# Tap spectra in steps of twelve output channels instead of eight

## The chip, the cores and the metric

The kernel runs on one core of a Trainium2 chip. The metric is device time in microseconds (us), the median of several runs. One further execution was recorded by the hardware profiler; all rows shown here come from its trace. The engines are named as the profile names them: PE (TensorE matmul) and PEld (its weight loads), DVE (VectorE), ACT (ScalarE), POOL (GpSimd) and SP (SyncE, which here only issues DMAs). Everything is fp32, and an fp32 matmul stands in the trace as two instructions (two passes).

## The reference, cut to what matters

There are two graph layers over 128 graphs of 128 nodes with 256 channels. The part that concerns the change is the convolution over 17 nodes in layer 0:

```python
h = relu(layernorm(x))                       # x: (128, 128, 256)
xc = transpose(h, (0, 2, 1))
h = relu(bn(conv1d(xc, conv1_w, 0)))         # 1 tap, 256 -> 256 channels
h = bn(conv1d(h, conv2_w, 8))                # 17 taps, padding 8, 256 -> 256
x_conv = transpose(relu(h + xc), (0, 2, 1))
...
```

Its result goes with a message-passing term into a GRU-like gate, and layer 1 (five graph convolutions over subsets of the first 25 nodes) follows. None of that is touched.

## The kernel before

The 17-tap convolution is done in the frequency domain. With a transform length of LW = 136, the signal and the taps are multiplied by cosine and sine tables (`fd` for the signal, `gt` for the taps), the spectra are multiplied frequency by frequency, and the result is transformed back. The span has these stages:

- The head stage, up to about 274 us. It runs over 32 blocks of four graphs (`heads`, L264). Block i makes the layer norm of a later block on DVE (`head_stats`, `head_norm`), the first convolution (`head_conv1`, L235 on PE, L238 on DVE, `head_relu` on ACT), the transposition of block i+1 (`head_turn`, L221 on PE, L222 on ACT, stored to DRAM as `htd`), and the signal spectra of block i-1 (`head_spectra`, L251 on PE, copied at L259 by DVE and L261 by ACT into `X`).
- Between these pieces, `between()` runs one tap step. `between` is `some_spectra`, which advances the generator `weight_spectra` (L165). The taps of conv2 come in 16 groups: two halves c of the input channels by eight groups q of WCH = 32 output channels. A group's taps `w2` hold four row groups (partitions 0, 32, 64 and 96 on, 17 rows each) with eight products each. A product takes 17 rows of taps for one output channel and 128 input channels as weights and streams the 136 columns of `gt` (L172). A step before does two products in each of the four row groups, eight output channels in all; the four row groups write four different PSUM banks, two products side by side in each (272 of a bank's 512 columns). Then the four banks are copied to the tile `sp`: three by ACT (L180), the fourth by DVE (L178), except in a group's last step, where ACT takes all four. A group has four steps, the whole has 64. When the generator is advanced once more, it stores `sp` (2,176 KB) to DRAM as `vd` (L182); the taps three groups on are then loaded, and the first step of the next group runs in the same call.
- The spectral stage, to about 457 us: for each of the 68 frequency pairs, `vd` is read back as `v`, POOL sums its real and imaginary parts (L324), and PE makes three products with `X` (L316, L327, L332).
- The gates and layer 1, to the end, with L658 the greatest part of PE's work.

In the head stage the order of the instructions on each engine is the program's own (`manual_schedule`), with a few small instructions of later code placed in between (the softmax of the fusion weights `fw`, L490 to L504, is one). PSUM is used in turn: `bank()` gives the eight banks in a fixed rotation, and so each allocation waits for whatever was to be read from the bank eight allocations before. A block with two steps takes 16 banks: one for each half of conv1, four for each step, two for the transposition and four for the signal spectra.

Four calls of `some_spectra` lie ahead of `heads`; in `heads`, each block has two calls (L271 and L288), and every eighth block a third one (L291). With 64 steps the last one falls into the early call of block 28, and the late call of that block issues the last store. All loads and stores of the head stage other than two small ones are issued by SP, in program order. `sp` has two buffers, `w2` three.

Of the kernel before, what the change touches and what calls it, by code (L numbers as in the profile page):

```python
# [13 lines left out]
P = 128  # L14
EPS = 1e-5
KW = 17
PAD = 8
BB = 4
LW = P + PAD
NP_ = LW // 2  # L20
NB = 20
WCH = 32
NR = LW - P
PARTS = [40, 40, 40, 8]
NN = 25
# [49 lines left out]
def gnn_kernel(ctx: ExitStack, tc: tile.TileContext, io, out0: bass.AP, out1: bass.AP):  # L75
    nc = tc.nc
# [13 lines left out]
    def bank():  # L90
        pool, n = banks
        if n is None:
            return pool.tile([P, 512], F32, tag="bank", name="bank")
        banks[1] = (n + 1) % 8
        return pool.tile([P, 512], F32, tag=f"bank{n}", name="bank")
# [56 lines left out]
    htd = [dram.tile([P, C, T], F32, tag=f"ht{i}", name=f"htd{i}") for i in range(NBLK)]  # L152
    vd = dram.tile([C, D // WCH, P, LW, WCH], F32, tag="vd", name="vd")
    yd = dram.tile([B, P, D], F32, tag="yd", name="yd")
    yrd = dram.tile([B, NR, D], F32, tag="yrd", name="yrd")

    def taps_load(pool, c, q, queue, split=1, amid=None):
        w2 = pool.tile([P, WCH // 4, P], F32, tag="w2", name="w2", bufs=3)
        for t in range(0, WCH // 4, WCH // 4 // split):
            queue.dma_start(w2[:, t:t + WCH // 4 // split], io["w2t"][:, c, q, t:t + WCH // 4 // split])  # L160
            if amid:
                amid.pop()()
        return w2

    def weight_spectra(pool, c, q, w2):  # L165

        sp = pool.tile([P, LW, WCH], F32, tag="sp", name="sp", bufs=2)
        for t in range(WCH // 8):
            ps = [bank() for _ in range(4)]
            for j in range(2):  # L170
                for r in range(4):
                    nc.tensor.matmul(ps[r][:, j * LW:(j + 1) * LW], w2[32 * r:32 * r + KW, 2 * t + j, :],  # L172
                                     gt[32 * r:32 * r + KW, :], start=True, stop=True)
            for r in range(4):
                o0 = t * 8 + 2 * r
                dst, s = sp[:, :, o0:o0 + 2], ps[r][:, :2 * LW].rearrange("p (j d) -> p d j", j=2)
                if r == 3 and t < WCH // 8 - 1:
                    nc.vector.tensor_copy(dst, s)  # L178
                else:
                    nc.scalar.copy(dst, s)  # L180
            yield
        nc.sync.dma_start(vd[c, q], sp)  # L182
# [4 lines left out]
    def head_load(pool, ahead, i, queue):  # L187
        xs[i] = pool.tile([P, BB, D], F32, tag="ln", name="ln", bufs=ahead)
        queue.dma_start(xs[i], x[i])
# [36 lines left out]
    def head_conv1(wk, i, h):  # L226
        if not h:
            h1s[i] = wk.tile([P, BB, D], F32, tag="h1", name="h1", bufs=2)
        ht = hcs[i]
        ps = bank()  # L230
        pv = ps.rearrange("p (b d) -> p b d", b=2)
        for bb in range(2):
            b = 2 * h + bb
            for c in range(C):
                nc.tensor.matmul(pv[:, bb, :], ht[:, c, b * N:(b + 1) * N], wc1[:, c, :],  # L235
                                 start=c == 0, stop=c == C - 1)
        hv = h1s[i][:, 2 * h:2 * h + 2, :]
        nc.vector.tensor_tensor(hv, pv, sh1[:, None, :].to_broadcast([P, 2, D]), op=ALU.add)  # L238

    def head_relu(i, h):  # L240
        hv = h1s[i][:, 2 * h:2 * h + 2, :]
        nc.scalar.activation(hv, hv, AF.Relu)
# [21 lines left out]
    def heads(wk, xk, ahead, X, between, consts):  # L264

        for i in range(NBLK + 1):
            if i + ahead < NBLK:
                head_load(xk, ahead, i + ahead, nc.sync)
            if i < NBLK:
                head_conv1(wk, i, 0)  # L270
            between()  # L271
            if i < NBLK:
                head_relu(i, 0)
            if i == 0:
                head_norm(1)
            elif i + 3 < NBLK:
                head_stats(wk, i + 3, (0,))
            if i < NBLK:
                head_conv1(wk, i, 1)
            if i + 1 < NBLK:  # L280
                head_turn(wk, i + 1)
            if i < NBLK:
                head_relu(i, 1)
            if i == 0:
                head_stats(wk, 2)
            if i + 2 < NBLK:
                head_norm(i + 2)
            between()  # L288
            if i > 0:
                head_spectra(X, i - 1)  # L290
            if i % 8 == 7:  # L291
                between()
            if i + 3 < NBLK:
                head_stats(wk, i + 3, (1,) if i else (0, 1))
            if i == 2:
                next(consts)
# [180 lines left out]
    def load_y(i):  # L477
# [4 lines left out]
        for o in range(C):  # L482
            for h in range(2):
                r0, g1 = 32 * (2 * o + h), g0 + 2 * h
                nc.sync.dma_start(yr[r0:r0 + 2 * NR, :],
                                  yrd[g1:g1 + 2, :, o * P:(o + 1) * P].rearrange("g r o -> (g r) o"))
# [22 lines left out]
    def conv_out(i):  # L509
# [5 lines left out]
        for o in range(C):  # L515
            for h, ps in enumerate(pss[o]):
                r0 = 32 * (2 * o + h)
                g = slice(r0, r0 + 2 * NR)
                nc.tensor.matmul(ps, yr[g, :], idr[g, :], start=True, stop=False)  # L519
# [602 lines left out]
def _spectral_constants():  # L1122
# [28 lines left out]
    for b in range(2):  # L1151
        idr[:, b * NR:(b + 1) * NR, b] = inv[P:]
    d = {"gt": gt.reshape(P, LW), "fd": fd.reshape(P, LW), "idm": inv[:P], "idr": idr.reshape(P, 2 * P)}
# [3 lines left out]
def _lay_out(a):  # L1157

    import numpy as np

    cc = np.ascontiguousarray

    def cols(v):
        return v.reshape(-1, P).T

    w = {k[7:]: v for k, v in a.items() if k.startswith("L0_gnn_")}
    l = {k[7:]: v for k, v in a.items() if k.startswith("L1_gnn_")}
    by = (-1, BB, P)
    d = {"x": cc(a["x"].reshape(*by, 2 * P).transpose(0, 2, 1, 3)), "xT": cc(a["x"].reshape(-1, BB * P, 2, P).transpose(0, 3, 2, 1)), "adjT": cc(a["adj"].reshape(*by, P).transpose(0, 3, 1, 2))}
    d["vec"] = cc(np.concatenate(  # L1170
        [cols(w[f"bn{j}_{q}"]) for j in (1, 2) for q in "gbmv"]
        + [cols(w["b_ih"]), cols(w["b_hh"]), cols(l["b1"]), cols(l["b2"])], axis=1))
    d["wc1"] = cc(w["conv1_w"][:, :, 0].T)

    w2 = w["conv2_w"].reshape(-1, WCH // 8, 4, 2, 2, P, KW).transpose(2, 6, 4, 0, 1, 3, 5)
    d["w2t"] = np.zeros((4, 32) + w2.shape[2:], np.float32)
    d["w2t"][:, :KW] = w2
    d["w2t"] = d["w2t"].reshape(P, 2, -1, WCH // 4, P)
    d.update(_spectral_constants())
    pad = np.zeros((2 * MW - w["w_msg"].shape[0] - 3, w["w_msg"].shape[1]), np.float32)  # L1180
    d["wms"] = cc(np.concatenate([w["w_msg"], w["w_se"], pad]).T)
    d["bms"] = cc(np.concatenate([w["b_msg"], w["b_se"], pad[:, 0]]))
    d["wih"] = cc(w["w_ih"].T)
    d["whh"] = cc(w["w_hh"].T)
    d["w1"] = cc(l["W1"])
    d["w2"] = cc(l["W2"])
    d["fw"] = cc(l["fusion_w"])
    sub = []
    for s, runs in GROUPS:
        idx = [r0 + j for r0, rn in runs for j in range(rn)]  # L1190
        sub.append((idx, a["adj"][:, idx][:, :, idx]))
    nblk = a["adj"].shape[0] // BB

    e = np.zeros((nblk, BB, NN, GW), np.float32)
    ie = np.zeros((BB, NN, GW), np.float32)
    bl = np.zeros((nblk, BB, NN, GW // BB), np.float32)
    fl = np.zeros((nblk, GW, NN), np.float32)
    for g, (idx, ad) in enumerate(sub):
        s = len(idx)
        ad = ad.reshape(nblk, BB, s, s)  # L1200
        for b in range(BB):
            c0 = GOFF[g] + b * s
            e[:, b, idx, c0:c0 + s] = ad[:, b].transpose(0, 2, 1)
            ie[b, idx, c0 + np.arange(s)] = 1.0
            fl[:, c0:c0 + s, :s] = ad[:, b]
            bl[:, b, idx, GOFF[g] // BB:GOFF[g] // BB + s] = ad[:, b]
    d["adjE"] = e.reshape(nblk, BB * NN, GW)
    d["ie"] = ie.reshape(BB * NN, GW)
    d["adjB"] = cc(bl.reshape(nblk, BB * NN, GW // BB).transpose(1, 0, 2))
    d["adjF"] = cc(fl.reshape(-1, P, NN).transpose(1, 0, 2))  # L1210

    d["adjN"] = np.zeros((len(PACKS), P, P), np.float32)
    d["adjK"] = np.zeros((P, len(PACKS), NN), np.float32)
    for j, (k, (g, b0, nb)) in enumerate(PACKS):
        s = len(sub[g][0])
        for b in range(nb):
            ad = sub[g][1][sum(PARTS[:k]) + b0 + b]
            d["adjN"][j, b * s:(b + 1) * s, b * s:(b + 1) * s] = ad.T
            d["adjK"][b * s:(b + 1) * s, j, :s] = ad
    return d  # L1220
# [22 lines left out]
```

## Time and profile before

| | us |
|---|---|
| median of 3 runs | 1865.76 (1865.35 to 1867.79) |
| the profiled execution | 1866.29 |
| its span, first to last instruction | 1864.5 |
| outside the span | 1.8 |
| head stage (to the first L316 product) | 273.6 |
| PE busy in the tap steps (L172), 1,024 instructions | 50.6 |
| ACT busy in the copies of the tap steps (L180), 208 | 67.0 |
| DVE busy in the copies of the tap steps (L178), 48 | 21.0 |

Busy times of a group are unions: where instructions overlap, the time counts once. The chain of waits is followed back from the last instruction to what released each step; its rows are start, length and the work. A row of PE matmuls in the timeline counts instructions, so that `x16` at L172 is a step of eight products in two passes each. The mean granted clock of TensorE over the span is 0.997: two short stretches ran at half clock, 33.45 to 36.86 us and 456.7 to 463.5 us, and PE's first products (up to about 20 us) take twice as long as later ones though the granted clock in the records is 1.0 there.

### The profile page before, as it was taken

Reading aid. Unit: us, or ns where it says so; the run is one execution under the profiler, and the core shown is the slowest. Engines: PE = TensorE matmul, PEld = TensorE weight load, DVE = VectorE, ACT = ScalarE, POOL = GpSimd, SP = SyncE. Lnnn points to the kernel's source line nnn. Section 1 sums busy time; section 2 is a strip of 40 time slices with the busy share of each in tenths; the row PEclk is TensorE's granted clock in tenths of the full one; section 3 lists DMA queues with packets and bytes.
Section 4 is the critical chain, followed back from the end, with each engine's and each line's share of the span. In section 5 each row is a group of like instructions: output and inputs, shape, how many; then the busy total and the mean of one; then the engine's idle time right before and its main releaser. Section 6 shows DMA issues by size and latency. Waiting matters only on the chain.

```text
span 1864.5 us, 31417 instructions
## 1 busy us (share of the span) xinstructions
PE 1843.8 (99%) x10982; PEld 1592.3 (85%) x10982; DVE 1361.9 (73%) x3312; ACT 737.0 (40%) x1668; POOL 652.9 (35%) x803
## 2 busy tenths in 40 slices
PE   8999999999999999999999999999999999999998
PEld 6888888887888888888888888888888888888887
DVE  6888865555988888888656778888756788888643
ACT  4666651111443334333334433433343343334334
POOL 1111125675343544454321345444412243544200
PEclk9999999999999999999999999999999999999999
DMA  8788778997532233224234422333232433222125
GB/s 294 285 303 334 302 277 285 344 325 244 171 88 75 72 85 94 76 73 124 73 90 119 120 75 72 88 83 113 61 103 85 131 95 87 73 72 70 39 89 158
DMA packets 219420, 267.98 MB, mean 144 GB/s; under 512 B 106210, under 2 KB 182967, under 8 KB 217215
## 3 DMA queue, kind: packets, MB, share of 16 engines
q1 hardware_dynamic: 214079, 248.04, 42.8%
q10 hardware_dynamic: 5184, 17.93, 2.4%
q8 instruction: 88, 1.44, 0.3%
q14 instruction: 69, 0.57, 0.1%
HBM read 169.24 MB, written 96.67 MB: 143 GB/s over the span
## 4 chain that ended last, share of the span: by engine, by line
PE 90%; DVE 4%; DMA 2%; POOL 2%; SPq 1%; issue 1%; ACT 1%; ACTq 0%; DVEq 0%; POOLq 0%
PE bank L658 43%; PE bank L332 6%; PE bank L235 6%; PE bank L926 5%; PE bank L986 5%; PE bank L544 4%; PE bank L251 4%; PE bank L523 3%; PE bank L327 3%; PE bank L609 3%; PE bank L172 2%; PE bank L221 1%; PE bank L905 1%; DMA nt<-in_adjN_dram 1%; PE bank L835 1%; PE bank L519 1%
## 5 line engine op out<-in xcount | busy, mean ns | idle before, releaser
L658 PE MATMUL bank<-t,sw 128*128 128x256 f32 x1152 | 291.4, 380 | 0.0
L671 POOL TENSOR_TENSOR u<-u,m 128x256 f32<-128x256 f32 x128 | 93.7, 732 | 465.1 <-ACT m L669 386.7
L658 PEld LDWEIGHTS bank<-t,sw 128*128 128x128 f32 x1152 | 212.7, 190 | 29.0 <-issue 2.3
L658 PE MATMUL bank<-t,wih 128*128 128x256 f32 x768 | 197.2, 379 | 0.0
L658 PEld LDWEIGHTS bank<-t,wih 128*128 128x128 f32 x768 | 145.5, 190 | 20.9 <-issue 0.9
L235 PE MATMUL bank<-wc,ht 128*128 128x256 f32 x512 | 126.0, 390 | 0.0
L324 POOL TENSOR_TENSOR vs<-v 128x256 f32<-128x256 f32 x134 | 99.0, 763 | 70.9 <-DMA v<-vd 44.1
L658 PE MATMUL bank<-t,whh 128*128 128x256 f32 x384 | 117.5, 388 | 0.0
L567 ACT ACTIVATE msg<-msg 128x512 f32<-128x512 f32 x64 | 36.9, 622 | 196.7 <-DVE msg L563 196.7
L658 PE MATMUL bank<-xc,wih 128*128 128x256 f32 x384 | 114.4, 379 | 0.0
L658 PE MATMUL bank<-xn,wih 128*128 128x256 f32 x384 | 114.2, 379 | 0.0
L986 PE MATMUL bank<-w,hh 128*125 128x256 f32 (+9 forms) x480 | 113.5, 380 | 0.6 <-DVE hh L931 0.6
L658 PE MATMUL bank<-ht,whh 128*128 128x256 f32 x384 | 109.9, 380 | 0.0
L205 POOL TENSOR_TENSOR rs<-ve,mhalf 128x4 f32<-128x4 f32 x32 | 32.3, 1009 | 217.0 <-DVE ve L203 209.9
L926 PE MATMUL bank<-ax,w 128*128 128x500 f32 (+8 forms) x416 | 107.0, 396 | 0.1
L235 PEld LDWEIGHTS bank<-wc,ht 128*128 128x128 f32 x512 | 93.8, 193 | 15.1 <-issue 0.3
L986 PEld LDWEIGHTS bank<-w,hh 128*125 128x125 f32 (+9 forms) x480 | 84.3, 178 | 18.8 <-DVE hh L931 1.0
L180 ACT COPY sp<-bank 128x272 f32<-128x272 f32 x208 | 67.0, 408 | 68.7 <-PE bank L172 52.9
L676 DVE TENSOR_TENSOR u<-bank,u 128x256 f32<-128x256 f32 x128 | 53.7, 420 | 54.6 <-PE bank L658 53.0
L321 DVE SCALAR_TENSOR_TENSOR s<-X 128x256 f32<-128x256 f32 x67 | 45.0, 672 | 64.9 <-PE bank L332 64.9
L669 ACT COPY m<-bank 128x256 f32<-128x256 f32 x128 | 47.3, 369 | 104.5 <-PE bank L658 104.5
L926 PEld LDWEIGHTS bank<-ax,w 128*128 128x128 f32 x416 | 69.9, 190 | 19.4 <-issue 12.3
(206 smaller groups left out, 4415.8 us busy)
## 6 DMA issues: line engine op xcount, KB each, us to landing
vd<-sp SPq DMA_DIRECT2D x16, 2176.0 KB
v<-vd SPq DMA_DIRECT2D x34, 1024.0 KB
w<-in_w_dram SPq DMA_DIRECT2D x40, 512.0 KB
ln<-in_x_dram SPq DMA_DIRECT2D x32, 512.0 KB
htd<-ht SPq DMA_DIRECT2D x32, 512.0 KB
yd<-ys ACTq DMA_DIRECT2D x32, 512.0 KB
ht<-htd SPq DMA_DIRECT2D x32, 512.0 KB
ym<-yd SPq DMA_DIRECT2D x32, 512.0 KB
```

Source lines behind the costliest of these rows:

```text
L180: nc.scalar.copy(dst, s)
L235: nc.tensor.matmul(pv[:, bb, :], ht[:, c, b * N:(b + 1) * N], wc1[:, c, :], start=c == 0, stop=c == C - 1)
L251: nc.tensor.matmul(ps[:, bb * LW:(bb + 1) * LW], h1[:, 2 * h + bb, c * P:(c + 1) * P], fd, start=True, stop=True)
L324: nc.gpsimd.tensor_tensor(vs[:, c], vr[c], vi[c], op=ALU.add)
L327: nc.tensor.matmul(p1[:, :D], a[:, c], vs[:, c], start=c == 0, stop=c == C - 1)
L332: nc.tensor.matmul(ps[:, k * D:(k + 1) * D], u[:, c], w[c], start=c == 0, stop=c == C - 1)
L523: nc.tensor.matmul(ps[:, b * N:(b + 1) * N], ym[:, 2 * h + b, o * P:(o + 1) * P], idm, start=False, stop=b == 1)
L544: nc.tensor.matmul(ps[:, b, :], d[:, b * N:(b + 1) * N], w, start=True, stop=True)
L658: nc.tensor.matmul(ps, w, d, start=n == 0, stop=n == len(pairs) - 1)
L671: nc.gpsimd.tensor_tensor(got["u4"], got["u2"], got["m5"], op=ALU.add)
L926: nc.tensor.matmul(pv[:, q - q0, :], w1s[k5 + g][:, c, q * P:(q + 1) * P], xv[:, c], start=c == 0, stop=c == C - 1)
L986: nc.tensor.matmul(ps[:n1, :D], hh[:, q, at:at + n1], w2s[k5 + g][:, q, :], start=q == 0, stop=q == HID // P - 1)
```

## The change

A step does three products in each row group, twelve output channels, and fills 408 of a bank's 512 columns. A group of eight products in each row group then has three steps, of 3, 3 and 2 products (48 steps in all, in place of 64), and its copies have 408, 408 and 272 columns. Output channels are assigned anew: row group r holds the eight consecutive channels from 8r on, so that a copy writes three (or two) neighbouring channels of `sp` for each frequency; the taps are laid out for this on the host. DVE takes the fourth bank in all but a group's last step, as before. The calls are thinned: the late call of a block runs in odd blocks and in block 0 only, and the third call of each eighth block is gone. The last step stays in the early call of block 28; the last store is then issued by the early call of block 29. The softmax of `fw` lies at other places between the early instructions of ACT and DVE, since the gaps that it is put into are others.

```diff
+STEP = 3
...
     def weight_spectra(pool, c, q, w2):
 
         sp = pool.tile([P, LW, WCH], F32, tag="sp", name="sp", bufs=2)
-        for t in range(WCH // 8):
+        n = WCH // 4
+        for s0 in range(0, n, STEP):
+            s1 = min(s0 + STEP, n)
             ps = [bank() for _ in range(4)]
-            for j in range(2):
+            for j in range(s1 - s0):
                 for r in range(4):
-                    nc.tensor.matmul(ps[r][:, j * LW:(j + 1) * LW], w2[32 * r:32 * r + KW, 2 * t + j, :],
+                    nc.tensor.matmul(ps[r][:, j * LW:(j + 1) * LW], w2[32 * r:32 * r + KW, s0 + j, :],
                                      gt[32 * r:32 * r + KW, :], start=True, stop=True)
             for r in range(4):
-                o0 = t * 8 + 2 * r
-                dst, s = sp[:, :, o0:o0 + 2], ps[r][:, :2 * LW].rearrange("p (j d) -> p d j", j=2)
-                if r == 3 and t < WCH // 8 - 1:
+                o0 = r * n + s0
+                dst = sp[:, :, o0:o0 + s1 - s0]
+                s = ps[r][:, :(s1 - s0) * LW].rearrange("p (j d) -> p d j", d=LW)
+                if r == 3 and s1 < n:
                     nc.vector.tensor_copy(dst, s)
                 else:
                     nc.scalar.copy(dst, s)
...
-            between()
+            if i % 2 or i == 0:
+                between()
             if i > 0:
                 head_spectra(X, i - 1)
-            if i % 8 == 7:
-                between()
...
-    w2 = w["conv2_w"].reshape(-1, WCH // 8, 4, 2, 2, P, KW).transpose(2, 6, 4, 0, 1, 3, 5)
+    w2 = w["conv2_w"].reshape(-1, 4, WCH // 4, 2, P, KW).transpose(1, 5, 3, 0, 2, 4)
```

## The prediction

> **What bounds the kernel now.** I read the engines' busy shares first, then the waits of PE, then the chain of waits in two stretches of the stage that the change touches, and last the rows of the tap steps.
>
> ```profile
> PE 1843.8 (99%) x10982; PEld 1592.3 (85%) x10982; DVE 1361.9 (73%) x3312; ACT 737.0 (40%) x1668; POOL 652.9 (35%) x803
> ```
>
> PE is never free. The changed code runs in the first 273.6 us (the head stage; the first product of the next stage, L316, starts at 273.57). The waits of PE in the whole span are few (the columns: microseconds in total, times, the longest), and those of the head stage lie nearly all in its first 34 us (of the two at L251, 0.6 ends at 33.5 and 0.4 at 51.7):
>
> ```profile
> PE bank L172 <- DMA gt<-in_gt_dram: 3.4, 1, 3.4
> ...
> PE bank L140 <- DVE bnb L136: 2.8, 1, 2.8
> PE bank L172 <- DVE h L238: 2.0, 1, 2.0
> PE bank L251 <- DVE h L238: 1.0, 2, 0.6
> ...
> PE bank L172 <- ACT sp L180: 0.5, 1, 0.5
> ```
>
> After 33.5 us the head stage is a row of PE work, so a PE microsecond removed there is a microsecond of the span. The chain of waits shows one block with two tap steps (L172):
>
> ```profile
> 99.71 2.05 PE bank L251 x16
> 101.77 1.73 PE bank L235 x8
> 103.49 0.68 PE bank L172 x16
> 104.17 1.92 PE bank L235 x8
> 106.09 0.87 PE bank L221 x8
> 106.97 0.68 PE bank L172 x16
> 107.64 2.05 PE bank L251 x16
> ```
>
> and, when the steps have run out, a block without any:
>
> ```profile
> 251.39 1.85 PE bank L251 x16
> 253.25 3.45 PE bank L235 x16
> 256.70 0.87 PE bank L221 x8
> 257.57 1.86 PE bank L251 x16
> ```
>
> The first period is 107.64 - 99.71 = 7.93 us, the second 257.57 - 251.39 = 6.18 us. Two steps cost 1.75 us, one costs 0.875 us: 0.68 under its own name, and 0.19 in the group behind it (L235 takes 1.92 behind a step and 1.73 elsewhere, L251 2.05 and 1.85).
>
> **What of it is work.** A step is 8 products of 17 rows by 136 columns, each of two passes, hence x16. Four of them, one in each row group, start within 0.02 us of each other in the trace, so a step is four rounds. The pass of L251 streams as many columns, and takes 1.85/16 = 0.1156 us. The cold start of the kernel gives the round separately, since one step and a pair of steps stand there:
>
> ```profile
> 3.37 1.29 PE L172 MATMUL bank<-gt,w 17*128 17x136 f32 x16 [3.37 <-DMA gt<-in_gt_dram]
> 9.43 2.20 PE L172 MATMUL bank<-gt,w 17*128 17x136 f32 x32
> ```
>
> Sixteen more cost 2.20 - 1.29 = 0.91, a round 0.228 us at half clock, 0.114 at full. I take 0.1155. Four rounds are 0.46 us of the 0.875, and 0.41 us is paid per step, however many rounds it has: the array empties before a step and after it.
>
> **What the Trainium skill says.** "TensorEngine Tiling (Array Packing)", section Key Properties: changing the tiling mode drains TensorE. That names the 0.41 us; the page gives no figure, and the trace agrees in that both neighbours of a step are longer. The same page, section PSUM Bottleneck, warns that tiling speeds up TensorE and not the evacuation; here ACT and DVE are next after PE, so I price them below. "TensorE: Matmul & The Clock Gate", section on the clock gate: the window that sets the clock is free-running, about 3.4 us. The trace has PE at half clock from 33.45 to 36.86 us, one such window, after the gaps of 2.0 and 0.6 us; where it falls can differ between executions.
>
> **The change part by part.**
>
> Where the steps go. Placement follows from the loop. Eight steps lie up to block 1, before and after. From there, before has 56 steps: one early in blocks 2 to 28 (27), one late in blocks 2 to 27 (26) and three extra ones. After has 40: the same 27 early ones, late ones in the 13 odd blocks 3 to 27. The last step lies early in block 28 in both, and from the store behind it on, the four queues of PE, ACT, DVE and SP hold the same instructions in the same order. So what is gained arrives whole at the next stage.
>
> PE. There are 256 rounds in both. The first eight steps have 32 rounds before, and 3,3,2,3,3,2,3,3 products, 44 rounds, after. In the part bound by PE: 16 steps fewer at 0.41 is 6.6 us; 12 rounds fewer at 0.1155 is 1.4 us. Sum 8.0 us.
>
> The first 33 us take these 12 rounds: six cold at 0.228 (1.37 us), six warm (0.69 us). They are hidden by PE's waits listed above, and the end of this part is set by DVE, at 33.46 us, when the h of L238 lets PE go on. DVE's own row there gains and loses little: the second step of block 0 is now the third of its tap group, whose copy is on ACT (0.35 us off DVE), and another copy is 0.14 us longer. Also, ACT's copies of the third step no longer stand behind the exponential that waits for fw until 13.78 us, which ended PE's wait at 14.80. If the cover holds I expect 0.3 us gained; if none of it hides anything, 2.1 us is lost; at best, with the half-clock window gone too, 2 us is gained (3.4 us at half clock are worth 1.7). I take 0.
>
> ACT and DVE.
>
> ```profile
> L180 ACT COPY sp<-bank x208: 370/406/478, 4.7 to 249.5; 128x272 f32<-128x272 f32 x104
> L178 DVE COPY sp<-bank x48: 428/436/444, 9.6 to 244.5; 128x272 f32<-128x272 f32 x48
> ```
>
> A tap group has 13 copies of 272 on ACT and 3 on DVE before; after, 6 of 408 and 4 of 272 on ACT, 2 of 408 on DVE: 3,536 and 816 columns, the same. Copies of 408 are not in the trace. Three of 272 in a row take 0.97 us on ACT, the last 0.40, so one starts every 0.284 us, 1.04 ns a column; 408 gives 0.43 us a copy, and 0.55 from start to end. The dearest view, by whole durations, is 0.61. On DVE 0.436 us plus 136 columns at 1.04 ns is 0.58.
>
> ```profile
> 100.00:200.00 100.00, 100.00 (x920) 85.13 (x918) 81.25 (x259) 60.68 (x185) 12.38 (x13) 1.00 0.85 325
> ```
>
> DVE is busy 81% of 7.93 us, 6.44 us, of which steps are 1.5 x 0.436 = 0.65. An even block now has 6.18 + 0.41 + 4 x 0.1155 = 7.05 us of PE, its one step is the third of the group and leaves DVE no copy: 5.8 of 7.05 us. An odd block has two steps of six rounds, 6.18 + 2 x 1.10 = 8.39 us, and DVE 5.8 + 1.16 = 6.95. Both keep DVE at 82 or 83%. No stage's average decides, though: the banks turn in rows of eight, and the late step of an odd block takes back three banks of the early one, 1.92 + 0.87 = 2.8 us after it (L235 and L221 lie between). ACT needs 0.2 + 3 x 0.43 = 1.5 us: cover 1.3 us. Cost 0; if the cover goes, the excess times 13.
>
> DMA. Bytes are the same, and the stage becomes 3% shorter; the share in the line above is 0.85. The store of a tap group now stands at each odd block, behind the x load of that block rather than before it: DVE's 2.9 us of waiting for ln can only shrink. The buffer sp is needed again one tap group (15.4 us) later, and a group with its neighbours on the queue, 3.7 MB at the 400 GB/s that the trace has in its busy stretches, needs 9 us. Cost 0. In the next stage POOL waits 44 us for v, but PE waits 0.2 us for POOL's sums, and the v loads start behind the same stores, so they move along with PE.
>
> Sum: 6.6 + 1.4 = 8.0 us. The profiled execution took 1866.29 us (span 1864.5 and 1.8 around it), so 1858.3; it lies 0.5 above the median of the runs, which gives 1857.8 us.
>
> **The rivals.**
> Partly eaten: in the 13 even blocks without a late step the turn of banks is faster, so DVE or ACT makes PE wait, say 0.25 us each: 3.3 us, leaving 4.7, 1861 us. For it: DVE stops for 2.6 us around block 3 (the constants wait for POOL), and PE lost 0.4 us there. Against it: 17% of DVE is free in either kind of block.
> Hidden anyway: the next stage is bound by its loads of v (DMA share 0.96 between 300 and 400 us), so an early start waits there, 1865 to 1866 us. Against it: PE is 100.00 busy in those 100 us, and loads wait for PE to free their buffers.
> Slower: ACT's wide copies are late for the banks of the late step in odd blocks. It decides from 0.87 us a copy ((2.8 - 0.2)/3); at 1.07 us PE waits 0.6 us in 13 blocks and the gain is gone; at 1.2 us it waits 1.0, 13 us in all, giving 1871 us. For it: three-column runs are in no row of this trace, and the section PSUM Bottleneck. Against it: ACT's time goes with the columns in every row (256 columns 0.37 us, 512 columns 0.60).
> That the change doesn't do what it says, I exclude: the order of instructions shows 48 steps.
>
> **How the numbers follow.** Forecast 0.79 (its own range 1855.5 to 1860), partly eaten 0.12, hidden 0.04, slower 0.05. The range of 1855.0 to 1861.6 takes in the unknown start (2 us either way), 1 us of scatter of the runs (they span 2.4 us) and most of the partly eaten case. A measurement of this kernel can tell 0.2%, 3.7 us, from no change: the forecast gives 0.43%. Faster 0.87 (forecast and most of partly eaten), same 0.07, slower 0.06.
>
> **What would show it.** Right: L172's successor has the same 1,024 instructions; a step of x24 takes 0.91 us in the chain, of x16 0.68; periods of 7.05 and 8.4 us alternate; the first v product starts near 265.5 us. Wrong: PE waits for ACT sp or DVE h after 40 us; steps of x24 above 1.0 us, which would make the round and not the switch the cost; or a wait at the first v product that takes the difference back.

## The result, and the profile after

The changed kernel takes 1857.34 us (median of 4 runs, 1855.81 to 1859.04) against 1866.74 us before (4 runs; three of them are in the table ahead of the prediction), a ratio of 0.995 with a 95% interval of 0.9933 to 0.9968. Run again later on one chip together with a better variant, it took 1861.04 us against 1868.01 (ratio 0.996, 0.9947 to 0.9973). So 7 to 9.4 us were gained where 8.0 were forecast. The profiled execution took 1857.39 us, its span 1855.6.

In every kernel from here on, the lines behind L20 have moved: the tap products are L175, conv1 L239, the transposition L225, the signal spectra L255, the first v product L319 (in the variants a few lines off).

The page's busy shares for the kernel after, first, and then its waits of PE (microseconds in total, times, the longest):

```profile
PE 1836.5 (99%) x10982; PEld 1590.0 (86%) x10982; DVE 1358.7 (73%) x3296; ACT 738.1 (40%) x1620; POOL 652.4 (35%) x803
```

```profile
PE bank L175 <- DMA w<-in_w2t_dram: 4.6, 2, 3.4
...
PE bank L175 <- DVE h L242: 1.3, 1, 1.3
...
PE bank L141 <- DVE bnb L137: 0.7, 1, 0.7
...
PE bank L255 <- DVE h L242: 0.5, 1, 0.5
```

PE has the same 10,982 instructions and is busy for 7.3 us less. Between 60 and 240 us it waits for nothing, as before. The chain of waits of after shows an even block (one step), an odd one (two), and an even one again:

```profile
102.51 1.86 PE bank L255 x16
104.37 1.73 PE bank L239 x8
106.09 0.91 PE bank L175 x24
107.00 1.92 PE bank L239 x8
108.93 0.87 PE bank L225 x8
109.80 0.91 PE bank L175 x24
110.71 2.05 PE bank L255 x16
112.76 1.73 PE bank L239 x8
114.48 0.68 PE bank L175 x16
115.16 1.92 PE bank L239 x8
117.08 0.87 PE bank L225 x8
117.96 1.85 PE bank L255 x16
```

A step of x24 costs 0.91 us, one of x16 still 0.68, and both leave 0.19 us in the group behind them. Two blocks take 117.96 - 102.51 = 15.45 us; two blocks of before with their four steps take 15.86. And the copies, from the groups of ACT and DVE at the tile `sp`:

```profile
L184 ACT COPY sp<-bank x160: 391/503/680, 6.7 to 239.6; 128x408 f32<-128x408 f32 x96, 128x272 f32<-128x272 f32 x64
L182 DVE COPY sp<-bank x32: 571/596/619, 9.5 to 234.4; 128x408 f32<-128x408 f32 x32
```

The first v product starts at 263.70 us in place of 273.57. Of these 9.87 us, 8.2 belong to what the forecast's sum put at 8.0. The other 1.7 are something that the sum left out: before had PE at half clock from 33.45 to 36.86 us, and this execution of after did not; half of these 3.41 us is lost time. The same twelve products behind the last wait of the start show 1.43 us of it (the rest is in the conv1 behind them, which takes 1.93 us in place of 1.73). Before, in the chain:

```profile
33.50 3.09 PE bank L251 x12
```

After:

```profile
33.51 1.66 PE bank L255 x12
```

Both executions leave the start at the same time, so the start itself gained nothing here. When after was run again, PE left the start at 32.85 us, the half-clock stretch was there (32.85 to 36.26 us), and the first v product started at 264.70. From that product to the end the two spans take 1590.9 us before and 1591.9 after, so the early start was not lost in the next stage.

### The profile page after: what moved, and what is told of

Its sections match the earlier page's. It is cut to its first block, busy times and chain, and to the rows that moved or that the text cites. A ratio compares the mean times of both kernels' runs of the same rounds, so it can differ in the third digit from the quotient of the medians.

```text
span 1855.6 us, 31339 instructions
## 1 busy us (share of the span) xinstructions
PE 1836.5 (99%) x10982; PEld 1590.0 (86%) x10982; DVE 1358.7 (73%) x3296; ACT 738.1 (40%) x1620; POOL 652.4 (35%) x803
## 4 chain that ended last, share of the span: by engine, by line
PE 93%; DVE 3%; DMA 2%; POOL 1%; SPq 0%; issue 0%; ACT 0%; ACTq 0%; DVEq 0%; POOLq 0%
PE bank L661 44%; PE bank L335 6%; PE bank L239 6%; PE bank L989 5%; PE bank L929 5%; PE bank L547 5%; PE bank L526 3%; PE bank L255 3%; PE bank L330 3%; PE bank L612 3%; PE bank L175 2%; PE bank L225 1%; PE bank L908 1%; PE bank L522 1%; PE bank L838 1%; DMA nt<-in_adjN_dram 1%
## 5 line engine op out<-in xcount | busy, mean ns | idle before, releaser
L239 PE MATMUL bank<-wc,ht 128*128 128x256 f32 x512 | 125.5, 389 | 0.0
L239 PEld LDWEIGHTS bank<-wc,ht 128*128 128x128 f32 x512 | 93.6, 192 | 14.7 <-ACT ht L226 0.3
L184 ACT COPY sp<-bank 128x408 f32<-128x408 f32 (+1 forms) x160 | 66.8, 511 | 70.2 <-PE bank L175 66.0
```

## The experiments

The theory: PE pays about 0.41 us each time it turns from the whole array to the row groups and back, however many rounds stand between the two turns; after has fewer turns. The rivals: the gain comes with the number of steps or copies, or with the layout, or with the call pattern.

Since the stages behind the head stage are untouched, yet took between 1590.9 and 1596.4 us in the profiles of this study, the start of the first v product is the sharper measure. The fourth column takes half of each half-clock stretch between 30 us and that start away from it. PE has the same 1,024 products at the tap line, and as many weight loads, in all these kernels but the whole array, so a price per product or per weight load would show no difference between them.

| kernel | ratio to before (95%) | first v product, us | at full clock, us |
|---|---|---|---|
| before | 1 | 273.57 | 271.9 |
| after | 0.995 (0.9933 to 0.9968) | 263.70 | 263.7 |
| after, again | 0.996 (0.9947 to 0.9973) | 264.70 | 263.0 |
| layout alone | 1.0003 (0.9994 to 1.0012) | 272.64 | 270.9 |
| steps of three, calls of before | 0.9962 (0.9948 to 0.9976) | 265.98 | 264.3 |
| pairs in odd blocks | 0.9967 (0.9954 to 0.998) | 265.49 | 260.4 |
| pairs of two | 1.0042 (1.0027 to 1.0057) | 282.30 | 275.5 |
| split steps | 1.0134 (1.0119 to 1.0149) | 296.74 | 295.0 |
| whole array | 0.9834 (0.9819 to 0.9849) | 242.97 | 243.0 |
| pairs from block 6 | 0.9928 (0.9913 to 0.9943) | 260.56 | 258.9 |
| pairs from block 6, again | 0.9928 (0.9916 to 0.994) | 260.02 | 258.3 |
| pairs in three of four blocks | 0.9986 (0.9978 to 0.9995) | 270.70 | 265.6 |

**One part alone: the layout.** From after:

```diff
-STEP = 3
+STEP = 2
...
-            if i % 2 or i == 0:
-                between()
+            between()
             if i > 0:
                 head_spectra(X, i - 1)
+            if i % 8 == 7:
+                between()
```

> The new channel layout alone: steps of two products and the calls of before. Theory (PE pays 0.41 us each time it turns from the whole array to the row groups and back, once per step): 64 steps as before, so the time of before, 1866.7 within 1.5 us, a step of x16 at 0.68 us in the chain, period 7.93. Rival (the gain comes from the layout, or from ACT and DVE writing neighbouring channels): the time of after, about 1857.

It takes the time of before (1867.95 against 1867.82 us), with a step of 0.68 us and a period of 7.92. The layout is worth nothing.

**One part alone: the width, with the calls of before.** The same diff without its first two lines.

> Steps of three products with the call pattern of before: two tap steps in every block, and a third in each eighth, until the steps run out near block 20. Theory: 48 turns wherever they stand, so the time of after, 1857.3 within 1.5 us. Rival (the thinned pattern is what lets banks and DVE keep up): PE waits for ACT sp or DVE h in blocks with two wide steps, 3 us or more above after.

1859.59 us, 2.3 above the 1857.3 of the forecast and so outside of its 1.5, though short of the rival's 3. At full clock its first v product starts 0.6 to 1.3 us behind those of after. Between 60 and 240 us PE waits for nothing, and the chain has the same 0.91 and 0.68 us. So the gain follows from the width; the thinned calls add about a microsecond at most.

**Double the suspected cost: split steps.** The steps, copies and banks of before, but the two products of each row group stand apart, with other work between (in `head_spectra` the hook `amid` runs behind its first half; the first eight steps stay whole):

```diff
                     nc.tensor.matmul(ps[r][:, j * LW:(j + 1) * LW], w2[32 * r:32 * r + KW, s0 + j, :],
                                      gt[32 * r:32 * r + KW, :], start=True, stop=True)
+                if not j:
+                    yield
...
+            if i > 1:
+                between()
...
-                head_spectra(X, i - 1)
+                head_spectra(X, i - 1, between if i > 1 else None)
```

> Steps of two products as before, same copies, same banks, but from block 2 on the two products of a row group stand apart with other work between them, so PE turns to the row groups twice in a step: 53 turns more, everything else of before. Theory: 53 x 0.41 = 22 us more than before, 1889, a half step of x8 takes 0.45 us under its own name. Rival (cost per step or per copy, whatever stands between): the time of before, 1867.

1892.1 us against 1868.08, 24 us more. One block in its chain of waits:

```profile
100.47 1.73 PE bank L241 x8
102.20 0.44 PE bank L175 x8
102.64 1.92 PE bank L241 x8
104.57 0.45 PE bank L175 x8
105.01 1.02 PE bank L227 x8
106.03 0.52 PE bank L175 x8
106.55 1.12 PE bank L257 x8
107.68 0.45 PE bank L175 x8
108.12 1.12 PE bank L257 x8
109.25 1.73 PE bank L241 x8
```

A half step of two rounds takes 0.44 to 0.52 us under its own name, where a step of four rounds took 0.68 and one of six 0.91: each round adds some 0.115 us to a fixed 0.22. Every group behind a half step is longer as well (the transposition 1.02 in place of 0.87). The period is 8.78 us with the work of 7.93: 0.425 us for each of the two added turns. At full clock the head stage is 23.6 us longer than the mean of before and the layout kernel, 0.445 us for each of the 53. With equal numbers of steps, copies, products and weight loads this rules out a price that goes with any of these; it goes with the visits to the row groups.

**Take the turn away: the whole array.** Two products over all 128 partitions stand for the eight of a step. The sums of the single row groups, three quarters of the tap spectra, are left out, and ACT makes all four copies.

```diff
-            ps = [bank() for _ in range(4)]
+            ps = [bank()] * 4
             for j in range(s1 - s0):
-                for r in range(4):
-                    nc.tensor.matmul(ps[r][:, j * LW:(j + 1) * LW], w2[32 * r:32 * r + KW, s0 + j, :],
-                                     gt[32 * r:32 * r + KW, :], start=True, stop=True)
+                nc.tensor.matmul(ps[0][:, j * LW:(j + 1) * LW], w2[:, s0 + j, :], gt, start=True, stop=True)
...
-                if r == 3 and s1 < n:
-                    nc.vector.tensor_copy(dst, s)
-                else:
-                    nc.scalar.copy(dst, s)
+                nc.scalar.copy(dst, s)
```

> The switch without row groups: each step makes its two products over all 128 partitions, into one bank, which ACT copies four times; the row groups' separate sums, and so three quarters of the tap spectra, are left out. The array streams as long as in a step of before (four passes of 136 columns, 0.46 us), but stays whole. Theory (the price is the turn between whole array and row groups): a step costs 0.46 in place of 0.875, 56 x 0.41 = 23 us less than before, 1844. Rival (any short group between longer ones pays at both ends): no gain, 1867.

1836.56 us, 31.5 less than before, and so more than forecast. The chain:

```profile
105.81 1.85 PE bank L250 x16
107.67 1.73 PE bank L234 x8
109.39 0.46 PE bank L174 x4
109.86 1.73 PE bank L234 x8
111.58 0.87 PE bank L220 x8
112.46 0.47 PE bank L174 x4
112.92 1.85 PE bank L250 x16
```

The step is 0.46 us, the four rounds and nothing more, and L234 behind it takes 1.73, L250 1.85, as where no step stands before them. The period is 7.11 against 7.93: 0.41 us for each turn. The surplus lies at the start: conv1 of block 2 begins at 28.37 us in place of 36.59, 8.2 us earlier (1.6 of them the half-clock stretch of before). DVE, which sets the end of the start, has none of its six copies of 0.43 us there; and PE leaves its slow first phase sooner (the eight conv1 products at 13.78 us take 2.05 us, those of before at 16.28 take 3.71). How much each of the two is worth was not tested. From there to the first v product it is 214.6 us against 237.0: 22.4 for 56 turns, 0.40 each. This kernel also has a quarter of the weight loads and one bank for each step in place of four, so it does not single out the turn by itself; the split steps, which change neither, do.

The Trainium skill's page "TensorEngine Tiling (Array Packing)", section Key Properties, says that changing the tiling mode drains TensorE. These two kernels agree in that each visit to the row groups has a price, 0.40 to 0.45 us for both ways. Whether all of it is draining no run here shows.

**Fewer turns with the same steps: pairs.** If turns are what is paid, two steps back to back pay once. In odd blocks both steps are put behind conv1, in even blocks the single one:

```diff
-            between()
+            if i < 2:
+                between()
...
                 head_conv1(wk, i, 1)
+            for _ in range(0 if i < 2 else 1 + i % 2):
+                between()
...
-            if i % 2 or i == 0:
+            if i < 2:
                 between()
```

> After, with the two steps of each odd block back to back behind conv1 (the even blocks' single step moved there too). Still 48 steps, 640 x 408/272 copies as in after, but from block 2 on 27 turns in place of 40. Theory: 13 x 0.41 = 5.3 us less than after, 1852, and 0.45 us less in each odd block (8.39 to 7.97). Rival (cost per step or per copy): 1857. Rival (banks): the second step waits for the first one's neighbours, PE bank L175 <- DVE h or ACT, and the gain is eaten.

(The number of copies there is a slip; it is 192 in both.) 1859.81 us: the 1852 of the forecast is missed and there is no gain in the whole, and yet both sides are in the trace. In the steady part two blocks take 15.09 us, from the chain below, 0.36 less than in after:

```profile
100.54 1.85 PE bank L255 x16
...
107.55 1.86 PE bank L255 x16
109.41 3.45 PE bank L239 x16
112.86 1.74 PE bank L175 x47
114.60 1.02 PE bank L225 x8
115.63 1.86 PE bank L255 x16
```

(The row x47 is the two wide steps, 48 instructions; they take 0.13 us more than 12 x 0.1155 + 0.22.) But in block 3, where DVE stops for POOL's power of the constants, L242 of both conv1 halves comes late, and the pair needs eight banks at once. The timeline of PE there:

```profile
46.80 1.20 PE L175 MATMUL bank<-gt,w 17*128 17x136 f32 x28
48.37 0.49 PE L175 MATMUL bank<-gt,w 17*128 17x136 f32 x2 [0.38 <-DVE h L242]
50.02 1.62 PE L175 MATMUL bank<-gt,w 17*128 17x136 f32 x18 [1.16 <-DVE h L242]
51.58 1.97 PE L225 MATMUL bank<-ident,ln 128*128 128x128 f32 x8
53.34 3.81 PE L255 MATMUL bank<-fd,h 128*128 128x136 f32 x16
```

The two waits are 1.5 us, and behind them PE runs at half clock from 50.16 to 56.99 us (L225 takes 1.97 in place of 1.04), 3.4 us more. With the stretch at 33 us, half clock costs this kernel 5.1 us, and the mean granted clock is 0.995 or 0.996 in all its five runs.

**The same with the steps of before.**

```diff
-STEP = 3
+STEP = 2
...
+            for _ in range(0 if i < 2 else 2):
+                between()
```

> Steps of two products as before (64 steps, 256 copies of 272), in back-to-back pairs behind conv1, 30 turns from block 2 on in place of 56. Theory: 26 x 0.41 = 10.7 us less than before, 1856, so as fast as after with none of its wider steps. Rival (cost per step or per copy): no gain, 1866.7. Rival (banks): part of the gain is lost in waits of PE for L238's h, up to 0.4 us in each block, 10 us.

1873.81 us: the rival of the banks is right. A pair should take 8 x 0.1155 + 0.22 = 1.14 us in the chain, and takes

```profile
114.82 1.51 PE bank L175 x32
```

since the fourth bank of the second step is that of conv1's second half, which L242 has just begun to read; the period is 7.85 us in place of 7.51. With only four rounds the first step is over too early; in the pairs of wide steps, whose first step has six, 0.13 us of this was left in place of 0.37. On top come longer waits for L242 (around block 3, and at 106 us behind a late load of x) and 6.8 us lost at half clock.

**Where the early waits are avoided.** After up to block 5, pairs from block 6 on:

```diff
-            between()
+            if i < 6:
+                between()
...
+            for _ in range(0 if i < 6 else 1 + i % 2):
+                between()
...
-            if i % 2 or i == 0:
+            if i < 6 and (i % 2 or i == 0):
                 between()
```

> After up to block 5; from block 6 on the two steps of an odd block back to back behind conv1, so that the stop of DVE around block 3 meets no pair. 11 turns fewer than after. Theory: in the first adjacent kernel each pair of blocks was 0.36 us shorter than in after, and 10.2 us at half clock, set off by the early waits, took it back; here 11 x 0.36 = 4.0 us less than after, 1853, with no half-clock stretch between 40 and 260 us. Rival (a pair costs elsewhere what it saves, say in DVE or DMA waits): 1857 or more.

1853.83 us, with no half-clock stretch between 40 and 260 us. To set it beside after, both were run on one chip:

> After once more, beside the kernel with pairs from block 6 on, on one chip. Theory: 8.0 us less than before by the turns and rounds, and up to 1.7 us more where the half-clock window of before at 33 us does not come: 8 to 10 us, ratio 0.9945 to 0.996.

> The pairs from block 6 on once more, beside after on the same chip. Theory: 11 turns fewer, 4.0 us less than after. Rival (the difference between two chips): no difference from after.

1853.41 us (1852.66 to 1859.37) against after's 1861.04 (1857.81 to 1863.73). The medians are 7.6 us apart; of that the head stage at full clock explains 263.0 - 258.3 = 4.7, near the forecast of 4.0, and the rest is in the stages that no kernel here changes (1594.4 and 1590.9 us in these two profiles); it is not counted as gain. The runs of the two kernels overlap a little (one of the five of after lies below two of the six), but over both pairs of profiles the head stage is 4.1 to 5.4 us shorter than in after.

**Still fewer turns.** All steps in pairs, in three of four blocks from block 6 on:

```diff
+            if i == NBLK - 3:
+                between()
+            elif i > 5 and i % 4 < 3:
+                between()
+                between()
```

> As the kernel with pairs from block 6 on, but every step in a pair, in three of four blocks: 17 turns in place of 34 in blocks 6 to 28 of after. Theory: 17 x 0.36 = 6.1 us less than after, 1851. Rival (the transfers become the bound: taps and their stores come in bursts): DVE waits for ln, then PE for h, 1857 or more.

1865.59 us, 14.6 above the forecast: nearly everything is given back. From its waits of DVE and its chain:

```profile
DVE st L203 <- DMA ln<-in_x_dram: 4.8, 5, 2.4
```

```profile
107.20 9.27 DMA ln<-in_x_dram
...
117.67 0.59 DVE h L242
...
118.30 0.72 PE bank L175 x10
```

A load of x is issued at 107.20 us behind a store of 2.2 MB and a load of taps, and lands at 116.47; DVE's statistics wait for it, L242 stands behind them, and the second step of the pair waits for L242's bank. The same chain stands before the waits at 149 and 214 us. PE loses 3.2 us in these three waits, and 5.1 at half clock (1.7 of them at 34 us, as in after's second profile). After has no wait of DVE for ln at all between 33 and 270 us. Pairs that begin with a narrow step also wait for L242, as in the pairs of two (x40 takes 1.74 us in place of 10 x 0.1155 + 0.22 = 1.37); there are six of them, 2.2 us together. These losses were not taken away one by one.

## Why the prediction was right

- The price per turn, 0.41 us, was taken from the two periods of before (7.93 and 6.18 us) less four rounds. Shown: 0.41 (periods) and 0.40 (whole stretch) by taking it away, 0.425 and 0.445 by doubling it.
- The round, 0.1155 us: a step of x24 was to take 0.91 us and takes 0.91.
- The sum of two blocks was to be 15.44 us and is 15.45. Its split into 7.05 and 8.39 was wrong, 7.25 and 8.20 from one L255 to the next: the 0.19 us that a late step leaves in the L255 behind it fall into the following block.
- The start, taken at 0: PE goes on at 33.51 us against 33.50, and at 32.85 in the second profile of after. One wait was not foreseen: the third product of the first step needs the second quarter of the first taps, and PE waits 1.25 us for it. It cost nothing because the wait for bnb shrank from 2.8 to 0.7 us.
- ACT and DVE at no cost: a copy of 408 columns takes 0.578 us on ACT (median of these alone; the estimate was 0.55) and 0.596 on DVE (0.58). The cover of 1.3 us held: in the blocks shown, ACT's three copies of the early step end at 108.32 us and the late step begins at 109.80. No PE wait for ACT is in the changed part. Behind block 3 there is one wait for L242, 0.5 us, where before had 0.4.
- DMA at no cost: DVE's waits for ln, 2.9 us, are gone, as the order on SP suggested.
- The size: the forecast was 1857.8 us and the measured median is 1857.34, closer than the sum deserves. The profiled executions differ by 8.9 us: 8.2 for the sum's 8.0, 1.7 more for the half-clock stretch at 33 us, which the sum put into the range only, and 1.0 less in later stages that were not touched. That the two nearly cancel is luck; in the second comparison the medians differ by 7.0. The first v product came at 263.70 and 264.70 us in place of 265.5. At full clock the head stage is 8.2 and 8.9 us shorter than before, 0.2 and 0.9 beyond the sum; in the second profile 0.65 of it is the earlier end of the start.

Of the rivals, none decided in after itself. The one that was named as slower, late evictions against the rotation of banks, is real and near: it took most of the gain of the pairs of two (0.37 us a block), with DVE's L242 and not ACT's wide copies as the late reader.

## What to carry to other kernels

Short groups of products in row groups pay a fixed price for each visit beside their work, here 0.41 us against 0.46 for four rounds. Compare the period of a loop with and without them, and not only the group's own time, since the group behind took nearly half of the price (0.19 us). Then make each visit as long as a bank allows, or put two visits together, provided that the banks which the second one needs have been read by then. An engine that is busy without a break can still have such time to give.

## What had not been expected of the hardware

- Half-clock stretches of PE came in steps of 3.41 us and followed waits much shorter than that: 0.38 and 1.16 us of waiting, within a stretch of slow tap steps, were followed by 6.83 us at half clock. Each 3.41 us at half clock cost 1.7, so that 1.5 us of waits cost 4.9. The Trainium skill's page "TensorE: Matmul & The Clock Gate", section on the HAM clock gate, speaks of at least one idle window of some 3.4 us before the clock falls; these traces show shorter gaps, and the measurement decides.
- The stretches begin on a fixed grid. Within each trace their starts lie whole multiples of 3.413 us apart (in the pairs kernel 33.09, 50.16 and 449.52). It is also the likeliest reason why the stretch at 33 us came in one profile of after and not in the other, with nearly the same waits of 1.3 and 0.5 us before it: laid back from the later stretches, the grid has a window from 29.44 to 32.85 us in the second profile, which holds both waits (1.78 us), while in the first it has a boundary at 30.91, inside the longer wait, which leaves 0.86 and 0.96 us in two windows. In the twelve traces, fourteen windows between 20 and 270 us have 1.17 us or more without a product, and all were followed by half clock; of the windows at full clock with less, only one was, with 0.80 us and a pair of tap steps in it. Near 440 us, however, two windows with 1.15 and 1.25 us were not, so the length of the waits is not the whole of it, and no run here moved the waits to test it.
- The clock records of the trace before begin at 19.8 us. The full clock that a view gives for the first 20 us therefore stands on no record, and the products there, which take twice as long, do not contradict it.
- The stages behind the first v product, equal in all these kernels, differed by up to 5.5 us between profiled executions (1590.9 to 1596.4), nearly as much as the change is worth.
